# The second expert stage of a decoder: weights loaded earlier, and the return summed by products into PSUM

## The chip, the cores and the metric

The kernel runs on one core of one Trainium2 chip. A core has five engines, which work side by side and wait for each other through semaphores: PE (TensorE, matrix products), DVE (VectorE), ACT (ScalarE), POOL (GpSimd) and SP (SyncE, which here only issues transfers). Transfers run on 16 DMA engines. The metric is device time in microseconds (us) of one execution.

## The reference, cut to what matters

Two decoder layers run on x of 8 batches of 256 tokens with 256 features. Each layer is a self-attention, a cross-attention and an expert stage, each added to its input and layer-normed. The change concerns the last expert stage and what stands just before it.

```python
x = _layernorm(x + _L1_attn_ref(x, ...))
x = _layernorm(x + _L1_xattn_ref(x, ctx_768, ...))
x = _layernorm(x + _L1_ffn_ref(x, gate_w, w1, b1, w2, b2))

def _L1_ffn_ref(tokens, gate_w, w1, b1, w2, b2):
    cap = int(1.25 * N / E)                      # N = 2048 tokens, E = 8, cap = 320
    probs = softmax(x @ gate_w.T)
    top2_w, top2_idx = top_k(probs, 2)           # two experts for each token
    counts = bincount(a_e, length=E)
    valid = (counts <= cap)[a_e]                 # an expert chosen too often gives nothing
    p = where(valid, minimum(pos, cap - 1), cap)
    buf = zeros((E, cap + 1, H)).at[a_e, p].set(x_a)
    h = silu(einsum('ech,efh->ecf', buf, w1) + b1[:, None, :])
    y = einsum('ecf,egf->ecg', h, w2) + b2[:, None, :]
    contrib = y[a_e, p] * (a_w * valid)[:, None]
    return contrib.reshape(N, 2, H).sum(axis=1)  # two weighted rows for each token
```

## The kernel before

All arithmetic is in float32; the tokens lie in x, 128 partitions by 16 chunks of 256 features, two chunks a batch. The program is a line of stages: a gated linear attention, a cross-attention, a first expert stage (`ffn0`), a self-attention (`self_attn`), a second cross-attention (`xattn`) and the second expert stage (`ffn1`). The attention stages are lists of steps that are run in rounds, each step on its own batch, so that several batches are under way at once; at a seam the last round of one stage alternates with the first rounds of the next. A scheduler of the framework then puts each engine's instructions in an order by its own model of their costs, within the dependencies; on the chip each engine works strictly in that order.

Memory for tiles comes from pools on two stacks, a left and a right one. A pool opened where another was closed must wait, tile by tile, for the last reader of what lay there. Self-attention keeps its queries, sums and outputs in a pool `s_tk` (L634), and the step `combine` (L901), which brings back the rows of the first expert stage while self-attention begins, has `c_wk` (L1289); both lie on the left. The two pools `s_kv` and `s_wk` (L632, L633) lie on the right, over what the first expert stage's weights left. When self-attention ends, the right side is emptied (L1298), and after the first rounds of the cross-attention the router of the second expert stage (`Route`, r1) is put there.

The router runs as steps of the cross-attention. `choose` writes each batch's rows to DRAM (L781, on SP) and ranks the experts, `place` and `enter` build the table of slots. After the last batch `ffn1` begins. Its weights w1 and w2 are loaded by 16 transfers on SP (L1317) and its biases b2 by 8 on ACT's queue (L1320), all issued behind the cross-attention.

`ffn1` has 2,560 slots (8 experts of 320), in 20 blocks of 128. For each block a gather on POOL (L896) fetches the tokens' rows, PE turns them (L1091) and DVE copies them out (L1092). `hidden` makes p_u by products with w1 and ACT applies Silu (L1103); `output` makes p_y by products with w2, DVE adds b2 (L1113), and POOL scatters the rows to a DRAM tensor ys (L1115), each to the place of its token and choice. When all scatters are down, the return begins. It runs over four groups of four chunks, in three functions, one group apart:

- `fetch_pair` reads the group's 8 rows a token back from ys in two transfers (L1145); ACT scales the first choice's row by its weight (L1155); POOL adds the residual x (L1157).
- `add_pair` adds the second choice's row times its weight on DVE (L1169) and takes the moments (L1173, L1174); a POOL instruction raises variance plus eps to the power -1/2 (L1176).
- `norm_pair` applies mean and deviation on ACT (L1184) and writes the output on SP (L1188).

The order in which a group's functions are called:

```python
for g in range(NG + 2):
    for f, n in ((fetch_pair, g), (add_pair, g - 1), (norm_pair, g - 2)):
        if 0 <= n < NG:
            f(n)
```

## Time and profile before

| | |
|---|---|
| median of 3 runs | 1300.39 us (1299.35 to 1302.56) |
| profiled execution, its own time | 1301.57 us |
| its span, first to last instruction | 1299.8 us |
| mean granted PE clock | 0.888 of full speed |
| busy: PE, DVE, ACT, POOL | 1054.2, 655.3, 448.4, 339.9 us |
| second cross-attention, from about | 1010 us |
| second expert stage, first gather | 1196.1 us |
| last scatter issued | 1261.2 us |

The profile is one execution seen by the hardware's own recorder. "L1157" is a line of the kernel. A line of the timeline gives start, duration, engine, line, operation, output<-input, and in brackets how long the engine idled before it and what released it. A line of the chain gives start, duration and what ran, followed back from the last instruction. A group's line gives busy time and the mean in ns of one instruction, and then the idle time before them with its releasers. PEclk is the clock that the throttle granted to PE, as a share of full speed. In float32 one product is recorded as two matmul instructions, so that x8 means four products.

### The profile page before, as it was taken

How to read it: one execution, taken by the hardware profiler on the slowest of the kernel's cores; microseconds unless marked ns; L12 is line 12 of the kernel's file. 1: busy time of each engine (PE TensorE's matmuls, PEld its weight loads, DVE VectorE, ACT ScalarE, POOL GpSimd, SP SyncE). 2: the span in 40 equal slices, each digit the busy share in tenths (PEclk: the TensorE clock that was granted, in tenths of full speed). 3: DMA queues.
4: the chain of work that ended last, by engine and by line, in shares of the span. 5: the costliest groups of instructions: out<-in, count | busy, mean ns of one | idle time of the engine just before them, and what ended most of it. 6: DMA issues, size and time to landing. Idle time of an engine off the chain costs nothing.

```text
span 1299.8 us, 25292 instructions
## 1 busy us (share of the span) xinstructions
PE 1054.2 (81%) x10221; PEld 692.1 (53%) x10221; DVE 655.3 (50%) x1833; ACT 448.4 (34%) x874; POOL 339.9 (26%) x454
## 2 busy tenths in 40 slices
PE   6888888888898649999997468888998888873870
PEld 4556665665665426666665235555555555652540
DVE  6667676654555432222222544444444566764325
ACT  3445454424444212212121134333443444330104
POOL 7545555430111021111111730000000110101544
PEclk9789988889999659999999689899999998975895
DMA  7000000003111291111111210000000010105425
GB/s 191 3 2 2 3 3 2 2 3 130 34 33 34 61 303 45 49 41 49 45 45 57 77 49 2 1 1 1 2 1 1 2 33 18 34 24 150 138 82 174
DMA packets 54517, 62.64 MB, mean 48 GB/s; under 512 B 10897, under 2 KB 45858, under 8 KB 54402
## 3 DMA queue, kind: packets, MB, share of 16 engines
q1 hardware_dynamic: 46368, 44.59, 10.6%
q0 software_dynamic: 5616, 15.34, 4.2%
q8 instruction: 82, 1.34, 0.4%
q10 hardware_dynamic: 2418, 1.09, 0.4%
q14 instruction: 33, 0.27, 0.1%
HBM read 42.78 MB, written 18.22 MB: 47 GB/s over the span
## 4 chain that ended last, share of the span: by engine, by line
PE 56%; DVE 24%; ACT 5%; POOL 5%; issue 4%; DMA 4%; SPq 0%; POOLq 0%; ACTq 0%; DVEq 0%
PE p_y L51 6%; PE p_u L1013 5%; PE p_y L1035 5%; PE p_v L1013 5%; PE p_pv L51 4%; DVE m L687 3%; PE p_q L51 3%; PE p_v L51 3%; PE p_s L681 3%; PE p_st L585 2%; PE p_k L51 2%; PE p_st L696 2%; DVE tot L267 2%; DVE al L275 2%; PE p_s L51 2%
## 5 line engine op out<-in xcount | busy, mean ns | idle before, releaser
L687 DVE TENSOR_REDUCE m<-p_s 128x2 f32<-128x512 f32 x128 | 80.1, 683 | 31.8 <-PE p_s L681 31.8
L1019 DVE TENSOR_TENSOR h<-h,p_v 128x512 f32<-128x512 f32 x39 | 26.8, 688 | 121.1 <-PE p_v L1013 121.1
L896 POOL DMA_INDIRECT xg<-rows,tok x39 | 37.0, 949 | 178.3 <-PE pt_g L1002 158.9
L122 DVE TENSOR_TENSOR y<-p_y,xb 128x512 f32<-128x512 f32 x24 | 16.5, 688 | 118.0 <-PE p_y L51 118.0
L1013 PE MATMUL p_u<-fw,xgT 128*128 x156 | 75.3, 606 | 0.6 <-DVE xgT L1004 0.6
L499 POOL TENSOR_TENSOR xb<-x,L_xattnbo 128x512 f32<-128x512 f32 x16 | 20.3, 1271 | 210.6 <-DVE y L122 169.6
L703 ACT ACTIVATE e<-p_st 128x512 f32<-128x512 f32 x128 | 66.9, 643 | 22.6 <-PE p_st L468 20.2
L1035 PE MATMUL p_y<-fw,hT 128*128 x312 | 73.8, 379 | 0.7 <-ACT hT L1028 0.7
L1013 PE MATMUL p_v<-fw,xgT 128*128 x156 | 74.0, 597 | 0.0
L1035 PEld LDWEIGHTS p_y<-fw,hT 128*128 128x128 f32 x312 | 59.2, 190 | 25.2 <-issue 18.2
L592 ACT ACTIVATE e<-p_st 77x512 f32<-77x512 f32 x128 | 65.7, 600 | 17.7 <-PE p_st L468 17.7
L1028 ACT COPY hT<-pt_h 128x512 f32<-128x512 f32 x39 | 22.8, 585 | 128.7 <-PE pt_h L1026 128.7
L477 ACT COPY u<-p_pv 128x512 f32<-128x512 f32 x48 | 28.1, 585 | 110.9 <-PE p_pv L51 109.9
L51 PE MATMUL p_pv<-e,vals 77*32 77x256 f32 (+1 forms) x1024 | 64.8, 394 | 0.0
L130 ACT COPY xT<-pt_x 128x512 f32<-128x512 f32 x40 | 23.4, 585 | 111.1 <-PE pt_x L129 110.5
L499 POOL TENSOR_TENSOR xb<-x,L_attnbo 128x512 f32<-128x512 f32 x8 | 10.1, 1268 | 189.4 <-DVE y L122 189.4
L129 PE MATMUL pt_x<-ident,x 128*128 128x128 f32 x160 | 28.2, 301 | 37.9 <-DVE x L115 37.5
L576 DVE TENSOR_REDUCE m<-p_s 128x4 f32<-128x308 f32 x128 | 53.0, 467 | 6.9 <-PE p_s L51 6.9
L51 PEld LDWEIGHTS p_pv<-e,vals 77*32 77x32 f32 (+1 forms) x1024 | 33.5, 112 | 32.0 <-issue 18.2
L1013 PEld LDWEIGHTS p_v<-fw,xgT 128*128 128x128 f32 x156 | 30.1, 193 | 38.2 <-issue 38.2
L681 PE MATMUL p_s<-kT,qT 32*128 32x512 f32 x256 | 50.0, 696 | 0.0
L260 POOL TENSOR_TENSOR kl<-kT,be 128x256 f32<-128x256 f32 x56 | 48.2, 861 | 4.4
(271 smaller groups left out, 2420.1 us busy)
## 6 DMA issues: line engine op xcount, KB each, us to landing
fw<-in_L_ffn_W SPq DMA_DIRECT2D x24, 512.0 KB
rows<-x SPq DMA_DIRECT2D x32, 256.0 KB
ys<-yo SPq DMA_DIRECT2D x39, 128.0 KB
m<-in_L_ffn_w SPq DMA_DIRECT2D x16, 256.0 KB
z<-ys SPq DMA_DIRECT2D x8, 512.0 KB
x<-in_x SPq DMA_DIRECT2D x8, 256.0 KB
out<-x SPq DMA_DIRECT2D x8, 256.0 KB
b<-in_L_ffn_b ACTq DMA_DIRECT2D x8, 128.0 KB
```

The lines of the kernel that those rows point to most:

```text
L51: nc.tensor.matmul(dst, l, r, start=(i == 0), stop=(i == n - 1))
L129: nc.tensor.transpose(pt[:, dc, c, :], x[:, 2 * b + c, dc * P:(dc + 1) * P], ident)
L260: nc.gpsimd.tensor_tensor(halves(kls[w][b % 2], w)[:, :, 0, :], halves(kT[b], w)[:, :, 0, :], halves(be, w)[:, :, 0, :], ALU.mult,)
L499: nc.gpsimd.tensor_tensor(xb, x[:, 2 * b:2 * b + 2, :], self.bo.unsqueeze(1).broadcast_to([P, 2, D]), ALU.add)
L576: nc.vector.tensor_reduce(st.less(b)[:, c, j, :], p, AX.X, ALU.max, negate=True)
L592: nc.scalar.activation(e[0:KV].rearrange("p i q -> p (i q)"), p[0:KV].rearrange("p i q -> p (i q)"), AF.Exp)
L681: nc.tensor.matmul(tiles[j].rearrange("p a m -> p (a m)"), st.qT[b][r, t, c * P:(c + 1) * P], kTs[b][r, t, :, :].rearrange("p a m -> p (a ...
L687: nc.vector.tensor_reduce(st.less(b)[:, c, j, 2 * t:2 * t + 2], p, AX.X, ALU.max, negate=True)
L703: nc.scalar.activation(e.rearrange("p i q -> p (i q)"), p.rearrange("p i q -> p (i q)"), AF.Exp)
L896: nc.gpsimd.indirect_dma_start(out=out, out_offset=None, in_=table, in_offset=bass.IndirectOffsetOnAxis(ap=index, axis=0),)
L1013: nc.tensor.matmul(p, xg[:, dc, :], w[:, bass.ds(e * (2 * FF) + dc * FF, FF)], start=(dc == 0), stop=(dc == 1),)
L1035: nc.tensor.matmul(y, hT[:, f * P:(f + 1) * P], w3[:, bass.ds(e * (4 * D) + f * D, D)], start=(f == 0), stop=(f == 3),)
```

## The change

It has three parts. The two pools `s_tk` and `c_wk` move to the right stack. The weights w1, w2 and the biases b2 are loaded there as soon as self-attention has left it, before the rounds of the cross-attention, and all of them on SP. The return is rewritten: while the expert products run, ACT multiplies the identity matrix by each token's weight (`spread`), which gives 32 diagonal matrices; the eight PSUM banks are filled with x by products with the identity; and each batch's returned rows are added there by products with the diagonal matrices. DVE takes the moments, and ACT the norm, from PSUM. The return works by batches of two chunks, with one read of 512 KB for each, all eight issued at once.

```diff
     def self_attn(w, masks, es, fs):
+        tk = es.enter_context(tc.tile_pool(name="s_tk", bufs=2, side="right", reuse_waits="tile"))
         kvp = fs.enter_context(tc.tile_pool(name="s_kv", bufs=1, side="right", reuse_waits="tile"))
         wk = fs.enter_context(tc.tile_pool(name="s_wk", bufs=2, side="right", reuse_waits="tile"))
-        tk = es.enter_context(tc.tile_pool(name="s_tk", bufs=2, reuse_waits="tile"))
...
+            by_weight = gp.tile([P, 2, NC, P], F32, tag="by_weight", name="by_weight")
+            def spread(n):
+                for k in range(2):
+                    nc.scalar.activation(by_weight[:, k, n, :], ident, AF.Identity, scale=wgt[:, k, n:n + 1])
...
                     if g:
                         output(5 * g - 5 + h)
+                        if 5 * g - 5 + h < NC:
+                            spread(5 * g - 5 + h)
...
-            (fetch_pair, add_pair, norm_pair and their loop)
+            back = ys[0:2 * NT, :].rearrange("(b c k p) d -> b p (c k) d", c=2, k=2, p=P)
+            for g in range(B):
+                z = wk.tile([P, 4, D], F32, tag="z", name="z", bufs=B)
+                s = nc.sync.dma_start(out=z, in_=back[g])      # waits for every scatter
+                zs.append(z)
+            for g in range(B):
+                p = ps.tile([P, 2, D], F32, tag="ps", name="p_z")
+                nc.tensor.matmul(
+                    p.rearrange("p c d -> p (c d)"), ident,
+                    x[:, 2 * g:2 * g + 2, :].rearrange("p c d -> p (c d)"),
+                    start=True, stop=False, skip_group_check=True,
+                )
+                sums.append(p)
+            def add_rows(g):
+                for c in range(2):
+                    for k in range(2):
+                        nc.tensor.matmul(
+                            sums[g][:, c, :], by_weight[:, k, 2 * g + c, :], zs[g][:, 2 * c + k, :],
+                            start=False, stop=(k == 1), skip_group_check=True,
+                        )
+            def moments(g):
+                for c in range(2):
+                    nc.vector.bn_stats(st, sums[g][:, c, :])
+                    nc.vector.bn_aggr(mv[:, c, :], st)
+                nc.vector.tensor_scalar(rs, mv[:, :, 1], EPS, None, ALU.add)
+                nc.gpsimd.tensor_tensor(rs, rs, mhalf[:, 0:2], ALU.pow)
+            def give(g):
+                nc.vector.scalar_tensor_tensor(nm, mv[:, :, 0], -1.0, rs, ALU.mult, ALU.mult)
+                for c in range(2):
+                    nc.scalar.activation(
+                        x[:, 2 * g + c, :], sums[g][:, c, :], AF.Identity, bias=nm[:, c:c + 1], scale=rs[:, c:c + 1]
+                    )
+                nc.sync.dma_start(out=out[S * g:S * (g + 1), :].rearrange(...), in_=x[:, 2 * g:2 * g + 2, :])
+            for g in range(B + 1):
+                for f, n in ((add_rows, g), (moments, g), (give, g - 1)):
+                    if 0 <= n < B:
+                        f(n)
...
-        ck = es.enter_context(tc.tile_pool(name="c_wk", bufs=2, reuse_waits="tile"))
-        steps = self_attn(w_s1, masks, es, fs)
+        ck = right.enter_context(tc.tile_pool(name="c_wk", bufs=2, side="right", reuse_waits="tile"))
+        steps = self_attn(w_s1, masks, right, fs)
...
         fs.close()
-        right.close()
         rest = round_of(steps, B)
         steps = xattn(w_x1, ctxT, 10000.0, xs)
         run(alternate(rest, round_of(steps, -2) + round_of(steps, -1)))
+        right.close()
         r1 = Route(1, wg1, rp, rw)
+        fw = right.enter_context(tc.tile_pool(name="ffn1_w", bufs=1, side="right", reuse_waits="tile"))
+        (m1, m2: 16 loads of 256 KB on SP; b2: 8 of 128 KB, now on SP too)
...
         for b in range(B + 2):
             run(round_of(steps, b))
-    (the same loads stood here, with b2 on ACT's queue)
     ffn1(r1, b1, b2, m1, m2, ys, dump)
```

More of the change, by code (lines that the diff above doesn't have):

```diff
@@ L1137, in ffn1 @@
                         output(5 * g - 5 + h)
-            back = ys[0:2 * NT, :].rearrange("(b c k p) d -> b p (c k) d", c=4, k=2, p=P)
-            yc, stats = {}, {}
-            def fetch_pair(g):
-                z = wk.tile([P, 8, D], F32, tag="z", name="z", bufs=4)
-                for h in range(2):
-                    s = nc.sync.dma_start(out=z[:, 4 * h:4 * h + 4, :], in_=back[g][:, 4 * h:4 * h + 4, :])
-                    for other in sent:
-                        tc.add_manual_dep(
-                            s.ins, other.ins.name,
-                            mybir.DependencyInfo(mybir.DependencyClass.Sync, mybir.DependencyReason.DATA),
-                            reason="any block may have written these rows",
-                        )
-                y = wk.tile([P, 4, D], F32, tag="yc", name="yc")
-                for c in range(4):
-                    n = 4 * g + c
-                    nc.scalar.activation(z[:, 2 * c, :], z[:, 2 * c, :], AF.Identity, scale=wgt[:, 0, n:n + 1])
-                for h in range(0, 4, 2):
-                    nc.gpsimd.tensor_tensor(
-                        y[:, h:h + 2, :], z.rearrange("p (c k) d -> p c k d", k=2)[:, h:h + 2, 0, :],
-                        x[:, 4 * g + h:4 * g + h + 2, :], ALU.add,
-                    )
-                yc[g] = z, y
@@ L1163, in add_pair @@
-            def add_pair(g):
-                z, y = yc[g]
-                mv = wk.tile([P, 4, 2], F32, tag="mv4", name="mv4")
-                rs = wk.tile([P, 4], F32, tag="rs4", name="rs4")
-                for c in range(4):
-                    n = 4 * g + c
-                    nc.vector.scalar_tensor_tensor(
-                        y[:, c, :], z[:, 2 * c + 1, :], wgt[:, 1, n:n + 1], y[:, c, :], ALU.mult, ALU.add
-                    )
+                        if 5 * g - 5 + h < NC:
+                            spread(5 * g - 5 + h)
@@ new lines, in ffn1 @@
+            back = ys[0:2 * NT, :].rearrange("(b c k p) d -> b p (c k) d", c=2, k=2, p=P)
+            zs, sums, stats = [], [], {}
+            for g in range(B):
+                z = wk.tile([P, 4, D], F32, tag="z", name="z", bufs=B)
+                s = nc.sync.dma_start(out=z, in_=back[g])
+                for other in sent:
+                    tc.add_manual_dep(
+                        s.ins, other.ins.name,
+                        mybir.DependencyInfo(mybir.DependencyClass.Sync, mybir.DependencyReason.DATA),
+                        reason="any block may have written these rows",
+                    )
+                zs.append(z)
@@ L1172, in add_pair @@
+            def moments(g):
+                mv = wk.tile([P, 2, 2], F32, tag="mv", name="mv")
+                rs = wk.tile([P, 2], F32, tag="rs", name="rs")
+                for c in range(2):
                     st = small.tile([P, 6], F32, tag="st1", name="st1")
-                    nc.vector.bn_stats(st, y[:, c, :])
+                    nc.vector.bn_stats(st, sums[g][:, c, :])
                     nc.vector.bn_aggr(mv[:, c, :], st)
                 nc.vector.tensor_scalar(rs, mv[:, :, 1], EPS, None, ALU.add)
-                nc.gpsimd.tensor_tensor(rs, rs, mhalf, ALU.pow)
+                nc.gpsimd.tensor_tensor(rs, rs, mhalf[:, 0:2], ALU.pow)
@@ L1177, in add_pair @@
                 stats[g] = mv, rs
-            def norm_pair(g):
-                (_, y), (mv, rs) = yc[g], stats[g]
-                nm = wk.tile([P, 4], F32, tag="nm4", name="nm4")
+            def give(g):
+                mv, rs = stats.pop(g)
+                nm = wk.tile([P, 2], F32, tag="nm", name="nm")
                 nc.vector.scalar_tensor_tensor(nm, mv[:, :, 0], -1.0, rs, ALU.mult, ALU.mult)
-                for c in range(4):
+                for c in range(2):
                     nc.scalar.activation(
-                        x[:, 4 * g + c, :], y[:, c, :], AF.Identity, bias=nm[:, c:c + 1], scale=rs[:, c:c + 1]
+                        x[:, 2 * g + c, :], sums[g][:, c, :], AF.Identity, bias=nm[:, c:c + 1], scale=rs[:, c:c + 1]
@@ L1186, in norm_pair @@
                     )
-                for h in range(4 * g, 4 * g + 4, 2):
-                    nc.sync.dma_start(
-                        out=out[P * h:P * (h + 2), :].rearrange("(c p) d -> p c d", p=P), in_=x[:, h:h + 2, :]
-                    )
-            for g in range(NG + 2):
-                for f, n in ((fetch_pair, g), (add_pair, g - 1), (norm_pair, g - 2)):
-                    if 0 <= n < NG:
+                nc.sync.dma_start(
+                    out=out[S * g:S * (g + 1), :].rearrange("(c p) d -> p c d", p=P), in_=x[:, 2 * g:2 * g + 2, :]
+                )
@@ L1305, in decoder_kernel @@
         r1 = Route(1, wg1, rp, rw)
+        fw = right.enter_context(tc.tile_pool(name="ffn1_w", bufs=1, side="right", reuse_waits="tile"))
+        m1 = fw.tile([P, NE, 2, D], F32, tag="m1", name="m1")
+        m2 = fw.tile([P, NE, 2, D], F32, tag="m2", name="m2")
+        for e in range(NE):
+            for t, n in ((m1, "L1_ffn_w1"), (m2, "L1_ffn_w2")):
+                nc.sync.dma_start(out=t[:, e, :, :], in_=a[n][e].rearrange("(c p) n -> p c n", p=P))
+        b2 = fw.tile([P, NE, D], F32, tag="b2", name="b2")
+        for e in range(NE):
+            nc.sync.dma_start(out=b2[:, e, :], in_=a["L1_ffn_b2"][e].partition_broadcast(P))
         steps.insert(len(steps) - 2, (r1.choose, -1))
@@ L1311, in decoder_kernel @@
         xs.close()
-    fw = right.enter_context(tc.tile_pool(name="ffn1_w", bufs=1, side="right", reuse_waits="tile"))
-    m1 = fw.tile([P, NE, 2, D], F32, tag="m1", name="m1")
-    m2 = fw.tile([P, NE, 2, D], F32, tag="m2", name="m2")
-    for e in range(NE):
-        for t, n in ((m1, "L1_ffn_w1"), (m2, "L1_ffn_w2")):
-            nc.sync.dma_start(out=t[:, e, :, :], in_=a[n][e].rearrange("(c p) n -> p c n", p=P))
-    b2 = fw.tile([P, NE, D], F32, tag="b2", name="b2")
-    for e in range(NE):
-        nc.scalar.dma_start(out=b2[:, e, :], in_=a["L1_ffn_b2"][e].partition_broadcast(P))
     ffn1(r1, b1, b2, m1, m2, ys, dump)
```

## The prediction

> **What bounds the kernel now.** I read the page first: PE is busy 81% of the span, but its row of slices falls to 3, 8, 7, 3 and 0 at the end, where the change lies. So the chain of waits over the last 135 us, then the timeline, the groups and the stretches of that part.

> ```profile
> 1186.35 6.07 DMA b<-in_L_ffn_b
> 1192.43 3.61 DMA m<-in_L_ffn_w
> ...
> 1197.43 7.21 DMA xg<-rows,src
> ...
> 1208.59 4.47 PE p_u L51 x8
> ...
> 1261.21 2.40 DMA ys<-yo,dst
> ...
> 1264.82 6.19 DMA z<-ys
> ...
> 1276.59 2.47 POOL yc L1157 x2
> 1279.06 2.13 issue
> ...
> 1286.79 1.27 POOL yc L1157
> ...
> 1288.09 1.87 DVE yc L1169 x2
> ```

> Two stretches are to be seen. At the head of the expert stage, gathers wait beside weight transfers. At the end PE has nothing to do, and the chain hops from a landing to POOL and VectorE.

> ```profile
> 1186.30 15.37 SPq L1317 DMA_DIRECT2D m<-in_L_ffn_w  x16
> 1196.07 1.06 POOL L896 DMA_INDIRECT xg<-rows,src  x1 [11.84 <-DMA m<-in_L_ffn_w]
> 1202.56 0.66 PE L1091 MATMUL pt_g<-ident,xg 128*128 128x128 f32 x2 [7.41 <-DMA xg<-rows,src]
> ```

> The first gather starts at 1196.07 and is used 6.5 us later. The index it needs left VectorE at 1195.8 (row L1061 of the timeline), so the DMA named as releaser only happened to end then: the transfers cost landing time, not start time.

> ```profile
> 1200.00:1204.00 4.00, 0.66 (x2) 0.29 (x2) 0.42 (x1) 0.00 (x0) 3.09 (x4) 0.50 1.02 342
> 1258.00:1260.00 2.00, 0.57 (x3) 0.16 (x1) 0.42 (x1) 0.00 (x0) 1.39 (x3) 1.00 0.18 66
> 1262.00:1264.00 2.00, 0.00 (x0) 0.00 (x0) 0.00 (x0) 0.00 (x0) 0.18 (x1) 0.50 0.18 66
> 1273.00:1275.00 2.00, 0.00 (x0) 0.00 (x0) 2.00 (x7) 1.36 (x4) 0.29 (x1) 0.50 1.11 349
> 1277.00:1279.00 2.00, 0.00 (x0) 0.00 (x0) 1.13 (x1) 0.00 (x0) 2.00 (x2) 0.50 0.21 67
> ```

> Stretches: PE, PEld, DVE, ACT, POOL busy, then PE clock, DMA share, GB/s. The DMA is full at 1200, and full again until about 1277.5, when the last returned rows land. The span ends 22 us after that: the end is bound by arithmetic passed between three engines.

> ```profile
> L1169 DVE SCALAR_TENSOR_TENSOR yc<-z,wgt,yc 128x256 f32<-128x256 f32 x16 | 10.6, 680 | 13.9 <-POOL yc L1157 13.8
> L1157 POOL TENSOR_TENSOR yc<-z,x 128x512 f32<-128x512 f32 x8 | 10.2, 1286 | 7.1 <-ACT z L1155 7.1
> L1184 ACT ACTIVATE x<-yc,nm,rs 128x256 f32<-128x256 f32 x16 | 8.3, 589 | 9.7 <-DVE mv L1174 5.4 <-DVE nm L1182 4.3
> L1173 DVE BATCH_NORM_STATS2 st<-yc 128x6 f32<-128x256 f32 x16 | 5.9, 412 | 0.0
> ```

> [...] clock 1.00 at 1258 to 1260, 0.50 from 1262 on, PE's last product ending at 1258.5; and at the head 0.50 until 1213.3 although PE worked from 1208.5. [...]

> **The change part by part.** In the instruction order of the two kernels, PE's differs only by one swap in the first self-attention round and by the new products at the end.

> *Weights and biases moved.* 16 issues of 256 KB and 8 of 128 KB, 5.24 MB, go to SP, ahead of the 16 row writes (L781). The first waits for DVE, PE, ACT and POOL: their last use of that memory is the norm of self-attention's batch 7, whose L115 ends at 1022.9. From there 5.24 MB at the 0.345 MB/us seen at 1200 take 15 us, or 24 issues at 0.96 us (15.37 by 16) take 23: done between 1038 and 1046, and the first row write issues at 1052.8. The cover is that gap of 7 us; if it is gone, the rows still have until 1196. Cost nothing. ACT loses 8 issues, none of which the chain waits for.

> *The head.* A gather in quiet is used 2.8 us after its start (712.28 to 715.07 in the chain of the combine). The fifth starts at 1201.21 (one each 1.26 us), so lands at 1204.0; its two transposes take 0.66 us and the copy 0.42, and the first p_u can start at 1205.2, not 1208.45. **-3.2 us**. Bounds: -1.0 if PE's half clock lasts longer for it; -5.2 if the PE gap of 2 us about 1217 goes too. POOL's 40 gathers and scatters at 1.27 us are 51 us, within the 66 they have now, so it follows.

> *Spreads.* 32 ACT instructions of 128x128. Rows of 128x16 (L797, 0.22) and of 128x256 (L1155, 0.50) bound one; I take 0.34, 10.9 us in all. ACT is 9.5 us busy of the 50 from 1210, so it fits; at most ten stand ahead of one hT copy, 3.4 us, and its products come a group of five blocks later. Cost nothing, at most +2.

> *The end.* Removed: 16 L1155 (7.1), 8 L1157 (10.2), 16 L1169 (10.6). Added on PE: 8 identity products of 512 columns and 32 of 256. PE's prices are in the old expert stage, where four products of 128x128 by 256 columns are eight records:

> ```profile
> 704.21 1.73 PE p_y L1035 x8
> ...
> 1177.61 3.79 PE p_y L51 x8
> ```

> 1.73 us at full clock, 3.79 in a stretch near half clock. The 512-column products take 0.86 each (chain: p_u L1013 x4, 1.72): 6.9 us, from 1258.5 to 1265.4, beside the last scatters. The first z lands at 1267.7, the others every 1.4 us. A batch needs 1.73 on PE; on DVE two L1173, two aggregates (0.17), two short ones, about 1.4; on ACT two L1184 at 0.52; POOL one pow of 0.71 (L113). So **PE becomes the bound** of the return: 1267.7 + 8 x 1.73 = 1281.6. PE idles 2.3 us before z, against 2.5 us from its last product to the clock's drop now; I take one half-clock window of 3.4 us, which loses 1.7: 1283.3. Bounds: 0 and 3.4. Then, for the last batch, stats 0.75, aggregates 0.23, add 0.19, pow with its hops 0.85, nm 0.2, two ACT 1.05: 3.3 us, to 1286.6. Today's last ACT ends at 1296.1, 3.7 us before the span: **end 1290.3, -9.5 us**. The new wait, PE for z, has nothing behind it on PE but later batches. nm of a batch waits for POOL behind the next batch's stats, and has their time. Stats and ACT read PSUM, for which no row stands: [...] I take the SBUF price.

> *Start of self-attention.* Its pools move, so three memsets of the cross-attention, done today before the combine's first gather, come after the fourth:

> ```profile
> 704.52 1.80 POOL L532 MEMSET vals<- 128x2048 f32 x1
> ```

> With two of 0.28 that is +2.4 us on POOL, which is full from 712 to 742 while PE waits 8.9 us for vals (L659), written in DVE's order. In return one gather less precedes each rs (-1.25). **+1.0 us**; bounds -1 and +4, as DVE's order of sums and maxima changes too. Fewer buffer waits on the first gathers could give 0.7.

> **Sum.** -3.2 - 9.5 + 1.0 = -11.7: span 1299.8 to 1288.1, profiled time 1301.57 to 1289.9. The median of runs lies 1.2 below the profiled one: 1288.7.

> **Rivals.** *More gain.* The clock stays up and the PE gap at 1217 was due to the load: -1.7 and -2.0 more, 1285; with no loss at self-attention 1284. For it: PE fills PSUM until just before z. Against: the gap at 1217 comes when the transfers are over, and 2.3 us of idling is close to what dropped the clock before.
> *The head gives nothing,* because the slow clock or the gathers' issue takes its place: 1291.9. Against: 6.5 us for a landing that takes 2.8.
> *The combine costs 4 us or more,* DVE being in order and PE waiting on it: 1292 to 1294.
> *Slower: PE at half clock through fill and return.* Place: 1258.5 to the end. Price: 8 x 1.9 + 8 x 3.79 = 45.5 us, to 1304.0, plus 7.0, less 2.2 of the other parts: span 1308.8, median 1309.4. With the fill fast and only the return slow, 1298.0 + 7.0 - 2.2: median 1303.4, no change that counts. It decides from the point where the return's products end after about 1295. [...]
> *The change isn't done,* weights waiting for a reader late in the cross-attention: this is the second rival's time.

> **How the numbers follow.** 0.3%, 3.9 us, is about what a measurement of this kernel can tell from no change. The forecast 0.55; more gain 0.15; no head 0.12; dear combine 0.08; half clock for the return alone 0.04, for all of it 0.06. Faster 0.90, same 0.04, slower 0.06. The range 1281.5 to 1296 leaves out the half-clock cases and the ends of the others, and takes in the bounds above with 1.5 us of spread.

> **What would show it.** Weight issues on SP at about 1023 and none at 1186; first pt_g near 1199.5, p_u near 1205; no POOL sums after the scatters; p_z products of 1.7 us a batch without gaps, with DVE waiting for PE; the last ACT near 1284.4 and the end 3.7 us after it. A return that follows landings at 1.4 us, or ends on DVE or POOL, or a head that starts no earlier, would make it wrong.

## The result and the profile after

The kernel after takes **1292.45 us** (median of 6 runs, 1288.96 to 1294.56) against 1300.34 for the kernel before in the same series (6 runs): ratio 0.9936, 95% interval 0.992 to 0.9951. It is faster by 7.9 us, where 11.7 were forecast. Its profiled execution took 1291.27, with a span of 1289.3. That is 1.2 below its own median, while the profiled execution of before was 1.2 above its own, so the two traces differ by 10.5 us and overstate the change by about 2.5. What follows compares stages of these traces.

First the chain of waits of the kernel after, from the expert stage's head to the second batch of the return (start, duration, what ran):

```profile
1204.19 2.75 DMA xg<-rows,src
...
1207.74 4.47 PE p_u L51 x8
...
1257.28 2.40 DMA ys<-yo,dst
1260.02 3.89 DMA z<-ys
1263.95 3.68 PE p_z L1172 x8
1267.65 0.76 DVE st L1182 x2
...
1268.92 0.72 POOL rs L1185
1269.67 0.16 DVE nm L1191
1269.83 0.67 DVE st L1182 x2
```

POOL's sums are gone after the scatters. But PE is on the chain with the first batch only, at half clock (granted 0.50 from 1263.95 to 1267.37; 3.68 for eight records). After that the chain hops DVE, POOL, DVE, one batch after another, to the end. (st are a batch's statistics, rs is POOL's power, and nm is minus the mean times rs, which ACT needs for the norm.) The groups of the last 35 us (busy time, mean ns | idle before, with its releaser) say who waits:

```profile
L1172 PE MATMUL p_z<-z,by_weight 128*128 128x256 f32 x64 | 15.8, 412 | 2.4 <-DMA z<-ys 2.4
L1182 DVE BATCH_NORM_STATS2 st<-p_z 128x6 f32<-128x256 f32 x16 | 6.1, 422 | 12.6 <-PE p_z L1172 12.6
L1191 DVE SCALAR_TENSOR_TENSOR nm<-mv,rs 128x2 f32<-128x2 f32 x8 | 1.3, 161 | 6.8 <-POOL rs L1185 6.8
```

DVE's statistics wait for PE once, before the first batch, and never again. DVE's nm waits 6.8 us in all for POOL's power, 0.80 to 0.87 in each batch, and the next batch's statistics stand behind it. The weights and the head, in the timeline:

```profile
1013.77 17.66 SPq L1319 DMA_DIRECT2D m<-in_L_ffn_w  x16
1031.87 7.01 SPq L1322 DMA_DIRECT2D b<-in_L_ffn_b  x8
...
1199.05 1.05 POOL L896 DMA_INDIRECT xg<-rows,src  x1 [12.31 <-DVE dst L1063]
...
1202.00 0.66 PE L1098 MATMUL pt_g<-ident,xg 128*128 128x128 f32 x2 [4.35 <-DMA xg<-rows,src]
```

One issue of the weights stands alone at 1013.8; the other 15 begin at 1022.4 and the biases follow until 1038.9. None is left at the head. A gather is now used 2.95 us after its start, not 6.5. But the first one starts 3.0 us later than before (1196.07): by then this execution has lost 3.0 us, most of the 3.8 that the head will win.

Every trace can be cut at the same points. The table gives the lengths in us:

- A, self-attention: from the last p_y of the first expert stage to the last p_y of self-attention;
- B, the second cross-attention with the router: to the start of dst, the list of places to which rows will be scattered;
- C: to the first gather;
- D, the head of the expert stage: to the first p_u;
- E, the expert products: to the end of the last scatter;
- F, the return: from the first use of a returned batch z to the end of the last ACT instruction;
- G: to the end of the span.

Before A, and between E and F, kernels differ by run or hardly at all.

| trace | A | B | C | D | E | F | G | span |
|---|---|---|---|---|---|---|---|---|
| before | 310.2 | 178.6 | 0.17 | 12.4 | 53.7 | 28.3 | 3.7 | 1299.8 |
| after | 312.3 | 178.6 | 0.65 | 8.6 | 50.7 | 22.1 | 3.3 | 1289.3 |
| after_again | 311.9 | 182.0 | 0.66 | 8.5 | 50.8 | 22.0 | 3.3 | 1291.6 |
| nm_later | 312.0 | 182.2 | 0.66 | 8.5 | 50.7 | 19.2 | 3.2 | 1291.1 |
| warm | 312.1 | 182.2 | 0.65 | 8.5 | 50.8 | 20.4 | 3.3 | 1292.0 |
| return_alone | 310.3 | 178.7 | 0.65 | 12.1 | 50.4 | 22.0 | 3.3 | 1291.0 |
| weights_alone | 312.6 | 178.6 | 0.74 | 8.6 | 61.1 | 28.3 | 3.7 | 1306.7 |
| memsets | 312.5 | 179.3 | 0.65 | 8.5 | 61.1 | 20.4 | 3.3 | 1299.7 |
| best | 312.5 | 179.2 | 0.65 | 8.5 | 61.2 | 17.5 | 3.3 | 1294.5 |
| before_again | 310.2 | 178.6 | 0.17 | 12.0 | 58.0 | 28.3 | 3.7 | 1306.5 |
| after_third | 313.1 | 179.1 | 0.65 | 8.5 | 61.1 | 20.4 | 3.3 | 1301.7 |
| best_same_chip | 312.3 | 178.6 | 0.65 | 8.6 | 59.6 | 17.5 | 3.2 | 1290.0 |
| best_head | 310.0 | 178.6 | 0.65 | 8.3 | 61.4 | 18.9 | 3.2 | 1293.1 |
| before_third | 310.2 | 177.6 | 0.17 | 12.0 | 54.0 | 29.0 | 3.7 | 1299.3 |

From before to after: A +2.1, C +0.5, D -3.8, E -3.1, F -6.3, G -0.4, the rest +0.5: -10.5.

### The profile page after: what moved, and what is told of

Its sections match the earlier page's. It is cut to its first block, busy times and chain, and to the rows that moved or that the text cites. A ratio compares the mean times of both kernels' runs of the same rounds, so it can differ in the third digit from the quotient of the medians.

```text
span 1289.3 us, 25471 instructions
## 1 busy us (share of the span) xinstructions
PE 1077.3 (84%) x10301; PEld 708.1 (55%) x10301; DVE 645.0 (50%) x1825; ACT 451.0 (35%) x890; POOL 331.4 (26%) x450
## 3 DMA queue, kind: packets, MB, share of 16 engines
q8 instruction: 83, 1.36, 0.5%
## 4 chain that ended last, share of the span: by engine, by line
PE 59%; DVE 23%; POOL 5%; ACT 5%; issue 4%; DMA 2%; SPq 1%; ACTq 0%; POOLq 0%; DVEq 0%
PE p_y L51 6%; PE p_u L1013 5%; PE p_y L1035 5%; PE p_v L1013 5%; PE p_pv L51 3%; DVE m L687 3%; PE p_q L51 3%; PE p_v L51 3%; PE p_st L696 3%; PE p_s L681 2%; PE p_st L585 2%; PE p_k L51 2%; DVE tot L267 2%; DVE al L275 2%; PE p_s L51 2%
## 5 line engine op out<-in xcount | busy, mean ns | idle before, releaser
L896 POOL DMA_INDIRECT xg<-rows,tok x39 | 37.0, 949 | 177.8 <-PE pt_g L1002 159.4
L1013 PE MATMUL p_u<-fw,xgT 128*128 x156 | 75.2, 605 | 0.6 <-DMA fw<-in_L_ffn_W 0.6
L1035 PE MATMUL p_y<-fw,hT 128*128 x312 | 73.8, 379 | 0.7 <-ACT hT L1028 0.7
L1013 PE MATMUL p_v<-fw,xgT 128*128 x156 | 73.3, 592 | 0.0
L1035 PEld LDWEIGHTS p_y<-fw,hT 128*128 128x128 f32 x312 | 59.2, 190 | 25.2 <-issue 18.2
L592 ACT ACTIVATE e<-p_st 77x512 f32<-77x512 f32 x128 | 65.7, 599 | 18.9 <-PE p_st L468 18.7
L51 PE MATMUL p_pv<-e,vals 77*32 77x256 f32 (+1 forms) x1024 | 64.0, 389 | 0.0
L499 POOL TENSOR_TENSOR xb<-x,L_attnbo 128x512 f32<-128x512 f32 x8 | 10.5, 1308 | 189.6 <-DVE y L122 187.8
L1013 PEld LDWEIGHTS p_v<-fw,xgT 128*128 128x128 f32 x156 | 29.8, 191 | 37.9 <-issue 37.9
L51 PEld LDWEIGHTS p_pv<-e,vals 77*32 77x32 f32 (+1 forms) x1024 | 33.3, 111 | 31.4 <-issue 16.9
L129 PEld LDWEIGHTS pt_x<-ident,x 128*128 128x128 f32 x160 | 18.6, 151 | 56.6 <-issue 23.8
```

What stands on the lines that cost most here:

```text
L51: nc.tensor.matmul(dst, l, r, start=(i == 0), stop=(i == n - 1))
L129: nc.tensor.transpose(pt[:, dc, c, :], x[:, 2 * b + c, dc * P:(dc + 1) * P], ident)
L499: nc.gpsimd.tensor_tensor(xb, x[:, 2 * b:2 * b + 2, :], self.bo.unsqueeze(1).broadcast_to([P, 2, D]), ALU.add)
L592: nc.scalar.activation(e[0:KV].rearrange("p i q -> p (i q)"), p[0:KV].rearrange("p i q -> p (i q)"), AF.Exp)
L896: nc.gpsimd.indirect_dma_start(out=out, out_offset=None, in_=table, in_offset=bass.IndirectOffsetOnAxis(ap=index, axis=0),)
L1013: nc.tensor.matmul(p, xg[:, dc, :], w[:, bass.ds(e * (2 * FF) + dc * FF, FF)], start=(dc == 0), stop=(dc == 1),)
```

## The experiments

They ran in three series, each beside the kernel before: 1300.14 (13 runs), 1304.22 (43) and 1305.12 (32) in the median. Each series had a chip of its own (1, 9 and 13), so a difference between series can be one between chips. The theory: the return is bound by the exchange between DVE and POOL, its first batch by PE's clock; self-attention loses by three memsets; the head gains its landing times. The rivals: PE or the landings bind the return; half-clock windows, and not the memsets, make self-attention longer; the return or the weights alone carry the gain.

**First series. The change again** (no edit).

> The changed kernel once more, for a second trace and more times. Theory: the 2.5 us that its first trace lost between the first expert stage and the second come from where single half-clock windows of PE fall (that trace shows 0.53 at 902 to 904 and 0.50 from 996 to 1000, after the same idle stretches of 1.5 us that left the clock at 1.00 in the kernel before), not from the pools; then this trace loses another amount there, between -1 and +3, and the runs spread over some 5 us about 1292.5. Rival: the moved memsets cost it; then 1.5 to 2.5 us are lost again, at the same two places and already before 842. In the return both expect 22.1 us from the first product with z to the last ACT, 2.06 to 2.19 a batch.

1293.33 us, ratio 0.9943 (0.9926 to 0.9961). F is the same. A loses 1.7 and B 3.4. PE has the same 1,312 matmul records in B as in the first trace. But from 1024.1 to 1034.4, near the start of B, the clock is at 0.50, where the first trace has 1.00: p_q (x4) and p_st (x16) take 1.81 and 1.94, against 0.92 and 1.03, and by then 2.7 us are lost. PE's waits just before are no longer than in the first trace (0.94 and 1.39, against 0.94 and 2.37), so nothing shows that the weights' transfers hold it up. B's 3.4 is mostly clock. A is taken up further down.

**The order of nm.**

```diff
+ m = nc.vector.scalar_tensor_tensor(nm, mv[:, :, 0], -1.0, rs, ...)
+ if g + 1 < B:   # in VectorE's order behind the add of eps of the next batch
+     tc.add_manual_dep(m.ins, last[g + 1].ins.name, NoSync ...)
```

> The changed kernel with one order: nm of a batch comes on VectorE behind the moments of the next batch. Theory: in the changed kernel VectorE waits 0.80 to 0.87 for POOL's power in each of 8 batches (6.8 us in all) with the next batch's stats behind that wait, and so sets 2.19 a batch; with the wait covered, PE is the bound again: 15.75 us of products (the first batch at half clock), then 3.3, so 19.1 from first product to last ACT in place of 22.1, -3.0: median 1289.5. Rival 1: landings of z or ACT set the pace, and nothing is gained: 1292.5. Rival 2: VectorE's own work of 1.4 a batch with its queueing takes the place, and half is gained: 1291.

1289.76 us, ratio 0.991 (0.9892 to 0.9927), 3.6 below the changed kernel of this series. F is 19.2, as computed. The group of nm in this trace, and the next batch's statistics:

```profile
L1182 DVE BATCH_NORM_STATS2 st<-p_z 128x6 f32<-128x256 f32 x16 | 6.1, 424 | 15.7 <-PE p_z L1172 15.7
...
L1191 DVE SCALAR_TENSOR_TENSOR nm<-mv,rs 128x2 f32<-128x2 f32 x8 | 1.2, 154 | 0.8 <-POOL rs L1185 0.8
```

Only the last batch's nm still waits for POOL (0.8), and the statistics wait 15.7 us for PE: PE is the bound, as the prediction had it for the whole return. Both rivals fall.

**PE kept busy until z.**

```diff
- nc.tensor.matmul(p_z[g], ident, x[batch g], start=True, stop=False)
+ for _ in range(1 + 3 * (g == B - 1)):
+     nc.tensor.matmul(p_z[g], ident, x[batch g], start=True, stop=False)
```

> The changed kernel with the last identity product repeated three times (2.6 us of PE, the same sums), into the 2.45 us in which PE waits for the first z. Theory: the clock stays at 1.00, the first batch's 8 records take 1.73 and not 3.68, and since VectorE starts from there, everything moves by 1.95, less 0.15 to 0.3 for the end of the repeated products: median 1290.8. Rival 1: the half clock comes from the work before, not from the wait, and the first batch stays at 3.7 or the drop comes a window later: 1292.5 to 1293. Rival 2: the repeated products run at half clock and push z's products back: 1294 or more.

1291.36 us, ratio 0.9923 (0.9901 to 0.9945); F 20.4, so 1.65 won. The first batch's half clock is no fixed part of the change, though. These are the return's products in after_again and then in memsets, a later run without this repair:

```profile
1266.28 15.77 PE L1172 MATMUL p_z<-z,by_weight 128*128 128x256 f32 x64 [2.41 <-DMA z<-ys]
```

```profile
1276.00 14.10 PE L1182 MATMUL p_z<-z,by_weight 128*128 128x256 f32 x64 [2.41 <-DMA z<-ys]
```

Both come after the same fill (the eight identity products, 7.03 us) and the same wait for z, 2.41. In after_again the first eight records take 3.65, at half clock; in memsets, and in after_third too, they take 2.01, and F is 20.4. So F is 22.0 with the half clock and 20.4 without it, 19.2 and 17.5 once nm is repaired. Why the same wait can do both is shown in the last section.

**The return without the early weights.**

```diff
- pools s_tk, c_wk on the right; w1, w2, b2 loaded before the cross-attention's rounds
+ pools and loads as in the kernel before
```

> The kernel before with the new return alone: pools, weights and biases as before. Theory: return worth 6.7 us here too (from z's first issue to the end 29.3 against 35.9), gathers as late as before (6.5 us from first gather to first pt_g): median 1293.6; PE's gap of 2 us at 1217 stays if it belongs to the weights' transfers, or is gone (-2) if it was an accident of one execution. Rival: the early weights carry the gain, and this gives less than 5: over 1295.5. Other rival: the moved pools cost 2.5 us at the start of self-attention, and without them this alone is as fast as the whole change: 1292 or less.

1295.09 us, ratio 0.9962 (0.9947 to 0.9978). F is worth 6.3 here too, D stays at 12.1, and A is 310.3: the pools do cost A. E is 50.4 with the weights still late, so the loads do not make the 53.7 of before. In medians of this series the early weights bring 1.8 (1295.09 to 1293.33), though the two intervals overlap.

**Second series. The early weights without the return.**

```diff
- ffn1 as in the kernel after
+ ffn1 as in the kernel before
```

> The kernel before with the moved pools and early weights alone; return as before, no spreads. Theory: from first gather to first p_u 8.5 us in place of 12.4 (-3.8), and 1.8 lost at the start of self-attention as in all four traces with the moved pools (312.1 against 310.2 from the last product of the first expert stage to the last product of self-attention): -2.0, median 1298.1. From the first p_u to the last scatter's end: 50.5 if the 53.7 of the kernel before was an accident of one execution, 53.7 if the old return's kernel brings it. Rival: the gain at the head is eaten whole by the start of self-attention and by half-clock windows in the cross-attention: 1299.5 to 1301.

1307.56 us against 1304.22: ratio 1.0021 (1.0009 to 1.0034), slower. D gives its 3.4 to 3.8 and A takes 2.4, as expected; but E is 61.1, and 58.0 in the kernel before of this series. The rival's result, by another cause, which is taken up below. So what the early weights bring as a whole is not settled: 1.8 gained beside the new return in one series, 3.3 lost beside the old one in another. Their own stage, D, gains in both.

**The memsets put behind the combine's gathers.**

```diff
- nc.gpsimd.memset(m, 0.0)
+ behind(nc.gpsimd.memset(m, 0.0))   # NoSync dependency on the last gather of combine
```

> The changed kernel with one order: POOL's three memsets for the cross-attention come behind the last of the 32 gathers of the combine, and no longer between the fourth and the fifth. Theory: they delay the fifth gather by 2.2 us (3.43 from fourth to fifth in place of 1.25), PE's first p_v of self-attention by 1.5, and so cost the 1.8 of that stage; without them the stage takes 310.2 to 310.5 again: median 1291.1. Rival: the stage is longer because the moved pools make other tiles wait, or because half-clock windows fall otherwise, and stays at 312: 1292.9.

1300.30 us against 1304.22, ratio 0.9966 (0.9955 to 0.9978). POOL's timeline at the first gathers of the combine, first of after_again, then of this kernel:

```profile
715.75 0.94 POOL L896 DMA_INDIRECT yg<-ys,idx  x1 [0.30 <-issue]
716.68 0.59 POOL L423 MEMSET mx<- 128x256 bf16 x2
717.18 1.83 POOL L532 MEMSET vals<- 128x2048 f32 x1
719.18 0.95 POOL L896 DMA_INDIRECT yg<-ys,idx  x1 [0.17 <-DVE yc L909]
```

```profile
717.35 0.94 POOL L906 DMA_INDIRECT yg<-ys,idx  x1 [0.30 <-issue]
718.60 0.94 POOL L906 DMA_INDIRECT yg<-ys,idx  x1 [0.30 <-issue]
```

From the fourth gather to the fifth it is 3.43 us with the memsets between, and 1.25 without. The p_v for which PE waits in self-attention (the stage's second, called the first in the expectations) comes 34.8 us after the last p_y began, as in the four traces with the old pools (34.8 to 34.9); in the six with moved pools and no repair it is 36.4. So the 1.5 is the memsets'. Yet A is 312.5 as a whole: up to its 210th us the stage is 0.4 ahead of the kernel before, and then it loses 2.7, with the clock at 0.75 and 0.82 from 932 to 940, where the kernel before has 1.00, and again about 996. The theory holds for the place and fails for the stage, and in the time nothing is seen of it: the ratio is that of after_third, 0.9967, which lacks this repair.

**All three repairs,** with the edits above.

> All three repairs in the changed kernel: nm behind the next batch's moments, the last identity product repeated three times, the memsets behind the combine's gathers. Theory: -3.0, -1.7 and -1.8 add, since they lie in a row: from the first product with z to the last ACT 13.8 + 3.3 = 17.1 to 17.5, with PE as the bound; self-attention 310.3; median 1286.4. Rival: with PE at full clock VectorE's 1.4 to 1.7 a batch or ACT is the bound, and the first two repairs give 3.5 together: 1287.6 or more; self-attention at 312: 1288 to 1289.

1296.87 us against 1304.22, ratio 0.9946 (0.9926 to 0.9966). F is 17.5, the lower bound that was computed. A is 312.5 again, in spite of the repaired memsets, and E is 61.2.

**The kernel before again.**

> The kernel before once more, for a second trace. Theory: the 2 us of PE gap at 1217 (53.7 us from the first p_u to the end of the last scatter, 50.4 to 50.8 in every kernel with the new return) were an accident of one execution: 50.5 here, so that they are no part of the change's gain. Rival: they belong to the kernel before, and 53.7 is seen again. Self-attention 310.2, return 28.3 from the first use of z to the last ACT.

One run of 1308.32 us. A and F agree with the first trace within 0.03; E is 58.0. Neither expected value: the gap in E is there, and larger.

**Third series. The change, the repairs, and PE kept busy at the head.** The fourth is the kernel before again.

```diff
+ for _ in range(3):
+     nc.tensor.matmul(p_w, ident, x[2 chunks])   # in PE's order behind the last p_tok
  for i in range(5):
      turn_rows(i)
+     if i < 4:
+         nc.tensor.matmul(p_w[:, 0:D], ident, x[1 chunk])
```

> The changed kernel a third time, beside the repaired ones. Question: between the first p_u and the last scatter's end, five traces of kernels with the new return show 50.4 to 50.8 us, but the four traces of the last series (the kernel before among them) 58.0 to 61.2, with ACT and VectorE waiting up to 9.5 us about 1217 to 1225 for results that PE had computed. Theory A: the stall belongs to the chip or the series; then all kernels of one series have it or none, and this trace agrees with the other three. Theory B: it belongs to the kernel; then this one shows 50.7 and the kernel before 53.7 or more. Without the stall 1292.5, with it about 1302.

> The three repairs again (order of nm, repeated identity product, memsets behind the combine's gathers), now in one series with the changed kernel. Theory: the return's repairs give 4.6 (17.5 in place of 22.1 from first z product to last ACT); the memsets give back 1.5 at the first p_v, which half-clock windows later in the stage may take again. So 4.6 to 6.1 below the changed kernel of this series: 1286.5 to 1288 without the stall. Rival: clock windows elsewhere eat it, less than 3.

> The three repairs, and besides, unused identity products on PE in the waits at the head: three of 512 columns before the first pt_g and one of 256 after each of the next four. Theory: they bring the clock back to 1.00 some 6 to 9 us sooner, at about 1202 to 1205, so the first p_u's 8 records take 2.3 in place of 4.6: -2.3 against the three repairs alone. If the stall after the first p_u hangs on the moment at which the clock comes back under load, it moves or goes. Rival: PE's products come 1 to 2 us late behind the unused ones, and nothing or +1 is left.

> The kernel before a third time, for its trace in this series: theory A expects here the same stall as in the changed kernel of the series (or none in both), theory B 53.7 to 58 here and 50.7 there.

after_third 1300.42 us (ratio 0.9967, 0.9951 to 0.9982), best_same_chip 1294.32 (0.9922, 0.9896 to 0.9948), best_head 1295.07 (0.9925, 0.9899 to 0.9951), before_third one run of 1301.04. The repairs are 6.1 below the changed kernel, the end of the expected 4.6 to 6.1, and **beat both kernels**; 1.5 of that lies in E (59.6 against 61.1), which the repairs were not meant to touch. With the busy head the clock is back at 1.00 from about 1198.6 and the first p_u's records take 2.40 in place of 4.62, as expected, and A keeps the whole 1.5 (310.0), but nothing is left in the time: E is 61.4, because PE resumes when it did without it (below), and F has a new wait of 1.12 for a z. A of 310.0 against 312.3, with the same edit to the memsets, goes with the clock: in A, half clock lasts for 17 windows of 3.41 us here and for 19 in best_same_chip.

## Why the prediction was right, and where it was not

The forecast was -11.7. The medians fell by 7.9 and the two traces differ by 10.5; 1292.45 is inside the range. The parts fit less well: the return gave 2.8 us less than was said, and the expert products, put at no change, 3.1 more. That the sum of the traces comes so close is luck, since these two have nothing to do with each other. And in the third series the changed kernel took 1300.42, above the range, and 4.7 below the kernel before.

- **The weights' move** cost nothing, as said: B is 178.6 in both first traces. (The 182.2 of three later ones is clock; see after_again.) All but one issue began at 1022.4 (1022.9 was said), and the DMA was idle again from about 1041, within 1038 to 1046; the first row write came at 1056.1.
- **The head** was put at -3.2 and gave -3.8 (D). The mechanism was right, landings without a load beside them: 2.95 us. C's +0.5 was in no term. In all eleven traces with any part of the change the first gather starts 0.47 to 0.56 after dst has ended; in the three of the kernel before it starts as dst ends, 0.3 after the index that it needs. Why it starts later is not shown.
- **Spreads** were put at nothing, and E of return_alone, which has them, is the shortest of all.
- **PE's term of the return** was right to 0.3: 13.84 plus 1.7 for a half-clock window, measured 15.75; without the window it is 14.1 (memsets), so the window cost 1.7. That one would fall there was a guess: it fell in four of the six traces with the fill unrepaired. The clock was at 0.50 from 1266.3 to 1269.7 in after_again, after 2.41 us of idling, and stayed at 1.00 after the same 2.41 in memsets. The window that the prediction put at 3.4 is 3.413 us in the traces (last section).
- **The step that failed** is the sentence "nm of a batch waits for POOL behind the next batch's stats, and has their time". The program's text has that order, but the scheduler's order on DVE is rs, nm, statistics: nm stands ahead of the next batch's statistics and holds them for POOL (0.80 to 0.87 us a batch), though these wait for PE no more. (An engine keeps its order in the traces: DVE's first 444 records and POOL's first 467 come in one order in before and after, though their starts differ by up to 1.0 and 1.1 us.) A batch so takes 2.06 to 2.19 and not PE's 1.73, and from first product to last ACT it is 22.1 and not 18.9. nm_later shows it: one edge in the order, 2.85 us. The prediction had compared PE's order in the two programs, and not DVE's.
- **Self-attention** was put at +1.0, bounds -1 and +4, for the memsets between gathers. They cost 1.5 at the p_v that waits (memsets shows it), and the stage is 1.7 to 2.9 longer in the traces with moved pools and no repair. The rest of that, and what the repair does not give back, goes with half-clock windows; no run holds the clock fixed, so their sizes are not shown apart.
- **E** was put at no change; the first pair gave -3.1, a gap in PE about 1217 that only the rival "more gain" and one bound of the head had. Their reason, the load, is not borne out, since return_alone loads late and has no gap. That gap is no steady part of the change.
- **The end's 3.7** fell to 3.3. Read from PSUM, the statistics take 422 ns each (412 from SBUF before) and ACT's norm 561 (589 before): that they cost about what they did from SBUF was the author's estimate, and it held.

Of the rivals, "the head gives nothing", "the combine costs 4 or more" and "the change isn't done" fall by D, A and the issues on SP; "half clock through fill and return", whose small weight was the author's estimate, lasted for one window.

## What to carry to other kernels

Price a new wait by what stands behind it in the engine's real order, not in the program's text: one edge of order was worth 2.85 us here, beside the 7.9 of the whole change. If a chain starts with PE after a wait such as the 2.41 us for z here, try filling the wait with harmless products: that saved 1.65 us here where the half clock fell without it, while in memsets and after_third it did not fall at all. And where PE waits as it does in self-attention here (0.68 and 1.11 us before one half-clock window), compare stages and several traces before a microsecond is put down to an edit: between after and after_again, the same kernel, B differs by 3.4 us, and most of that is clock.

## What the runs showed of the hardware

**The clock windows.** Stretches of 2 us in self-attention, of the kernel before and then of the kernel after (length; PE, PEld, DVE, ACT, POOL busy; then PE clock, DMA share, GB/s):

```profile
900.00:902.00 2.00, 0.89 (x6) 0.45 (x4) 1.80 (x9) 0.47 (x1) 0.00 (x0) 1.00 0.00 0
902.00:904.00 2.00, 2.00 (x18) 1.56 (x22) 0.00 (x0) 0.84 (x2) 0.00 (x0) 1.00 0.00 0
```

```profile
900.00:902.00 2.00, 0.89 (x7) 0.47 (x5) 1.70 (x9) 0.47 (x1) 0.00 (x0) 1.00 0.00 0
902.00:904.00 2.00, 2.00 (x9) 1.33 (x8) 0.00 (x0) 0.56 (x2) 0.00 (x0) 0.53 0.00 0
```

The same instructions, 0.1 us apart, after the same two idle stretches of 0.68 and 1.11 us: once the clock stays, once it halves, and 1.5 us are lost. Here waits of less than 1.2 us at a time were enough, which was not expected.

Where the boundaries fall is not settled by chance alone: the four traces with the old pools give A within 0.1 of each other (310.2 to 310.3).

**A stall in E, whose cause is open.** In all eight traces of the second and third series PE waits soon after the first p_u, for 2.7 to 9.8 us. The timeline of after_third, PE's turned rows first, then those that need them:

```profile
1218.51 0.82 PE L1098 MATMUL pt_g<-ident,xg 128*128 128x128 f32 x6
...
1225.06 0.53 ACT L1110 ACTIVATE hT<-p_u,b 128x320 f32<-128x320 f32 x1 [3.82 <-remote]
...
1226.48 1.09 DVE L1099 COPY xgT<-pt_g 128x256 f32<-128x256 f32 x3 [9.39 <-remote]
...
1227.00 2.47 PE L51 MATMUL p_u<-xgT,m 128*128 128x320 f32 x4 [7.67 <-issue]
```

The records have PE's products over by 1219.3, but DVE gets to copy them at 1226.5, with a releaser that the profile calls remote, and PE then waits in its turn. The ends of PE's records are modelled, so it is not excluded that PE itself was late. None of the five traces with the new return before those series has it (E 50.4 to 50.8). The kernel before has it in all three of its traces, in the first one too: there DVE's copies wait 6.6 to 7.1 us at this place. Against 50.6, the kernels before lose 3.1, 7.4 and 3.4, and the changed ones of the later series 9.0 to 10.8. It does not follow the moment at which the clock comes back: in best_head that is 5.3 us before the first p_u, in after_third and best_same_chip 4.8 and 5.2 after it, and PE resumes 16.2, 15.7 and 15.6 us after the first p_u. Neither the early loads nor the new return are needed for it, since before_again has neither. Whether it hangs on the chip, and why kernels with early weights lose more, was not settled. What the change is worth goes with it: 0.9936 and 0.9943 where the changed kernel was free of it, 0.9967 in the third series.
